# A gated recurrence on one core: h @ wh as sums of three bf16 numbers, the x side as plain products

## The chip, the core and the metric

The kernel runs on one core of one Trainium2 chip. The metric is the device time of one launch in microseconds (us); three runs of the kernel before gave a median of 1659.17 us (1657.54 to 1660.16).

## The reference

A recurrence over T = 512 steps for a batch of 8 with 512 inputs and 512 state units; all is float32.

```python
def step(h, x_t):
    fused = jax.nn.sigmoid(jnp.concatenate([x_t, h], axis=-1) @ w_W + w_b)
    hidden_state, output_state = jnp.split(fused, 2, axis=-1)
    memory_state = x_t @ wx_W + wx_b + hidden_state * (h @ wh_W + wh_b)
    h_new = output_state * h + (1.0 - output_state) * jnp.tanh(memory_state)
    return (h_new, h_new)
out = x + scan(step, cond_1024, x)
```

Below, r is the first gate (hidden_state), z the second (output_state). Each step needs four products with 512 x 512 matrices of the new state or input: h with the gates' two blocks, h with wh, x with the same three. Only the products with x can be made ahead of time.

## The kernel before, in words

**Layout.** State and inputs lie transposed, units on the 128 partitions, in four blocks k = 0 to 3 of 128 units; the contraction runs over k. Half A of the state is k = 0, 1, half B is k = 2, 3. Outputs are cut into four strips j of 32 PSUM partitions: a product (`mm`, L193) takes 32 columns of state as its stationary operand (8 of them hold the step's batch, the other 24 are zero, one group of 8 rows for each of four steps s) and streams the weights, so that four products, one for each strip j, stand side by side in the array. Four steps make a group g, with one set of PSUM banks for each of two groups in turn.

**A step on TensorE** (L372 to L384). `ORDER` (L27) names the groups of four products: A (192 columns: wh for half A, z and r for half A), B (128: r and wh of half B), C (64: z of half B), each for k = 0 to 3, in the order A0 B0 A1 A2 A3 B1 B2 B3 C0 C1 C2 C3. Then one slot of the x side's products for a later group (`take`, L384). The banks have been filled with the x side's sums by ScalarE copies (`spread`, L254), and the products add to them.

**The x side** (`products`, L293). For each pair of groups the 2 x 2 blocks of x and weights are combined as in a fast matrix product with seven products instead of eight: weight sums `tw` (`weight_sum`, L271, made once), x sums `sx` on POOL (`x_sum`, L282), and additions and copies on VectorE and ScalarE that put the parts together (L493 to L547), over eight steps in a hand-written order.

**A step on the other engines** (L458 to L483), for half A, then half B. VectorE transposes the gate's and wh's columns from PSUM to SBUF in 32 x 32 blocks (`turn_r`, `turn_h`, `turn_z`), ScalarE takes the sigmoids, and a scan on VectorE (`memory`, L447) multiplies and adds over two slots for each unit: r times (h @ wh), plus x's part. ScalarE's Tanh follows, and a second scan (`update`, L453) over three slots (h; n - h; times 1 - z plus h) gives the new state. `memory` and `update` are made for each block of 128 units, so twice in each half. All engines work in order. Two small memsets (`idle`, L432, L556) fill places of VectorE. ScalarE copies the state once more into the first slot (L483). POOL adds x to the state for the output (`add`, L557), SP loads x and stores the output in chunks of 16 steps (`load_x`, L106; `store`, L565), the last chunk in two parts.

The names and lines that the prediction uses: `mm` L194 (all matmuls), scans L390, sigmoid and Tanh L224, transposes L406 and L422, output additions on POOL L558, the x side's VectorE additions L495, L528, L534.

Of the kernel before, what the change touches and what calls it, by code (L numbers as in the profile page):

```python
# [16 lines left out]
B = 8  # L17
HU = 64

DVE_FILL = 23
IDLE = 3
LAST = 4
SYNC = mybir.DependencyInfo(mybir.DependencyClass.Sync, mybir.DependencyReason.DATA)

ORDER = "A0 B0 A1 A2 A3 B1 B2 B3 C0 C1 C2 C3"  # L27

FIRST = "A0 x A1 x A2 x A3 B0 B1 B2 B3 C0 C1 C2 C3"

BANKS = {"A": 192, "B": 128, "C": 64}

HALF = 192

WIDE = 384

SUMS = ((2,), (2,), (2, 1), (2, 1), (1,), (1, 3), (3,), (3, 3))

Q01, Q23 = slice(0, 64), slice(64, 128)

COLS = slice(64, 448)

XP = {"A": slice(0, 192), "X": slice(192, 320), "C": slice(320, 384), "B": slice(384, 512)}
# [3 lines left out]
def tile_cond_rnn_residual(  # L47
# [7 lines left out]
    wb3_d: bass.AP,  # L55
# [4 lines left out]

# [13 lines left out]

# [56 lines left out]

    wa = const.tile([P, NQ, NQ, 192], F32, name="wa")
    for k in range(NQ):
        nc.sync.dma_start(out=wa[:, k], in_=wa_d[k])
    wb = const.tile([P, NQ, NQ, 192], F32, name="wb")
    nc.sync.dma_start(out=wb[:, :3], in_=wb_d)
    nc.sync.dma_start(out=wb[:, 3], in_=wb3_d)

    def wh(bank, k, j):
        return wa[:, k, j] if bank == "A" else wb[:, k, j, {"C": slice(0, 64), "B": slice(64, 192)}[bank]]  # L140
# [3 lines left out]
    def pair(n, name, rows, slots):  # L144

        return const.tile([P, 2, rows, slots], F32, name=name).rearrange("p c n s -> p n c s")

    NH = 2 * GS  # L150
    hT = [[pair(n, f"hT{n}{i}", 32, 3) for i in range(NH)] for n in "AB"]

    md0 = [[pair(n, f"md0{n}{i}", 32, 2) for i in range(2)] for n in "AB"]
    md1 = [[pair(n, f"md1{n}{i}", 32, 2) for i in range(2)] for n in "AB"]
    hd0 = [[pair(n, f"hd0{n}{i}", B, 3) for i in range(2)] for n in "AB"]
# [11 lines left out]
    for n, t_ in enumerate(hd0[0] + hd0[1] + md0[0] + md0[1] + hT[0] + hT[1]):  # L167
        (nc.vector if n < DVE_FILL else nc.gpsimd).memset(t_, 0.0)
    for t_ in hd0[0] + hd0[1]:
        nc.gpsimd.memset(t_[:, :, :, 1], -1.0)  # L170
    idle = const.tile([P, IDLE], F32, name="idle")

    tw = [const.tile([P, 2, 2, WIDE], F32, name=f"tw{n}") for n in range(4)]
    sx = [[const.tile([P, 2, GS * B], F32, name=f"sx{n}{q}") for q in range(2)] for n in range(4)]
    step_bias = const.tile([P, HALF], F32, name="stepbias")
    xs = [const.tile([P, 512], F32, name=f"xs{n}") for n in range(2)]
    u2 = const.tile([P, WIDE], F32, name="u2")
    u3 = const.tile([P, WIDE], F32, name="u3")
    both = const.tile([P, WIDE], F32, name="both")

    def state(hf, i, slot=2):

        s = i % GS
        return hT[hf][i % NH][:, B * s : B * s + B, :, slot]

    ctx.enter_context(tc.manual_schedule())
    banks = [
        {n: psum.tile([P, w], F32, name=f"{n}{q}") for n, w in BANKS.items()}
        for q in range(2)
    ]  # L190
    xps = [psum.tile([P, 512], F32, name=f"xp{q}") for q in range(2)]

    def mm(out_, lhsT, rhs, start=False):  # L193
        nc.tensor.matmul(  # L194
            out_, lhsT, rhs, start=start, stop=False, skip_group_check=True
        )


    for t_ in list(banks[0].values()) + list(banks[1].values()):
# [10 lines left out]
    for t_ in xs:  # L210
        for c_ in (slice(0, 64), slice(448, 512)):
            nc.gpsimd.tensor_copy(t_[:, c_], bias[:, c_])
    for hf in range(2):
        for slot in (0, 2):
            nc.vector.tensor_copy(
                state(hf, 0, slot), hin[:, 2 * hf : 2 * hf + 2].rearrange("p c b -> p b c")
            )


# [9 lines left out]

    def seed(g):  # L230

        nc.scalar.copy(xps[g % 2][:, COLS], bias[:, COLS])

    def prefill(g):

        c, t0 = divmod(g * GS, TC)
        for k in range(NQ):
            for j in range(NQ):
                mm(
                    xps[g % 2][32 * j : 32 * j + 32, 64:448],  # L240
                    x_of(c, k, t0, GS),
                    wx[:, k, j, :],
                )
            yield

    def prefill_two():
        yield from prefill(2)
        yield from prefill(3)

    def source(g):  # L250

        return xs[g % 2] if g else xps[0]

    def spread(g, names):  # L254

        for n in names:
            nc.scalar.copy(banks[g % 2][n], source(g)[:, XP[n]])

    def turn_x(g, e):

        c0 = XP["X"].start + 32 * e
        nc.vector.transpose(md1[e // 2][g % 2][:, :, e % 2, 1], source(g)[:, c0 : c0 + 32])

    def wx_of(kh, nh):
        return wx[:, 2 * kh : 2 * kh + 2, 2 * nh : 2 * nh + 2]

    def x_half(o, n, kh):

        return x_of(o // 2, slice(2 * kh, 2 * kh + 2), 8 * (o % 2) + GS * n, GS)

    def weight_sum(n, k=slice(0, 2), j=slice(0, 2)):  # L271

        a, b = [
            (wx_of(0, 1), wx_of(0, 0)),
            (wx_of(1, 1), tw[0]),
            (wx_of(1, 1), wx_of(0, 1)),
            (wx_of(1, 0), tw[1]),
        ][n]
        at = (slice(0, P), k, j)
        nc.vector.tensor_tensor(tw[n][at], a[at], b[at], ALU.subtract)  # L280

    def x_sum(o, n):  # L282

        t_ = [q[o % 2] for q in sx]
        a, b, op = [
            (x_half(o, 1, 0), x_half(o, 1, 1), ALU.add),
            (t_[0], x_half(o, 0, 0), ALU.subtract),
            (x_half(o, 0, 0), x_half(o, 1, 0), ALU.subtract),
            (x_half(o, 0, 1), t_[1], ALU.subtract),
        ][n]  # L290
        nc.gpsimd.tensor_tensor(t_[n], a, b, op)

    def products(o):  # L293

        t_ = [q[o % 2] for q in sx]
        p1 = (0, x_half(o, 0, 0), wx_of(0, 0))
        p2 = (0, x_half(o, 0, 1), wx_of(1, 0))
        p3 = (0, t_[3], wx_of(1, 1))
        p4 = (1, x_half(o, 1, 1), tw[3])
        p6 = (0, t_[1], tw[1])  # L300
        p7 = (1, t_[2], tw[2])

        def pair(left, right, k, c0=0, c1=WIDE):
            for j in range(NQ):
                bank, lhs, rhs = left if j < 2 else right
                mm(
                    xps[bank][32 * j : 32 * j + 32, COLS.start + c0 : COLS.start + c1],
                    lhs[:, k],
                    rhs[:, k, j % 2, c0:c1],
                    start=right is p7 and k == 0 and j >= 2,  # L310
                )

        def shared(k):
            for j in range(NQ):
                c0 = HALF * (1 - j // 2)
                mm(
                    xps[j // 2][32 * j : 32 * j + 32, COLS.start : COLS.start + HALF],
                    t_[0][:, k],
                    tw[0][:, k, j % 2, c0 : c0 + HALF],
                )  # L320

        pair(p1, p7, 0)
        yield
        pair(p1, p7, 1)
        yield
        pair(p2, p6, 0)
        yield
        pair(p2, p6, 1)
        yield
        pair(p4, p3, 0, 0, 288)  # L330
        yield
        pair(p4, p3, 0, 288)
        shared(0)
        yield
        shared(1)
        pair(p4, p3, 1, 0, 96)
        yield
        pair(p4, p3, 1, 96)
        yield
# [7 lines left out]
    def x_side():  # L347
        for o in range(2, NG // 2):
            yield from products(o)

    seed(1)
    take(prefill(0))
    warm()
    later = x_side()
    first = {1: prefill(1), 2: prefill_two()}
    weight_sum(0)
    spread(0, "BCA")
    for e in range(NQ):
        turn_x(0, e)

    pool_done = {}
    summed = []
    for i in range(T):
# [5 lines left out]
        if t == 0:  # L369
            ot = out_p.tile([P, TC, NQ, B], F32, tag="ot", name=f"ot_{c}")  # L370

# [285 lines left out]
```

## Time and profile before

| | |
|---|---|
| runs, median of 3 | 1659.17 us |
| span of the profiled execution | 1659.2 us |
| that execution's first to last steady VectorE transpose of half A (510 steps) | 22.59 to 1654.18 us |
| DMA over the span | 31.16 MB, mean 19 GB/s |
| instruction fetch, largest queue | 424 packets, 6.95 MB |

The span runs from the first to the last instruction of one execution, and the durations used below are of that execution. PE is TensorE's matmuls and PEld its weight loads, which overlap them; DVE is VectorE, ACT is ScalarE, POOL is GpSimd, SP is SyncE, which issues most DMAs. A timeline row gives the start, the time from there to the group's end, the engine, the line, the operation, out<-in, sizes (partitions x elements, type), the count, and in brackets the idle time before it with what ended it. A f32 product leaves two matmul rows and two weight loads in the trace. Rows of one tile are merged, so a row with x8 covers eight matmuls of one k.

### The profile page before, as it was taken

To read this page: it belongs to the slowest core of one execution; us is meant where nothing else is said; L and a number is where in the kernel's file an instruction comes from. 1 tells how busy PE (TensorE), PEld (TensorE's weight loads), DVE (VectorE), ACT (ScalarE), POOL (GpSimd) and SP (SyncE) were. 2 spreads that over 40 slices of the span, in tenths; PEclk is the share of its full clock that TensorE was granted. 3 is DMA by queue.
4 is the path that set the end of the run, shared out by engine and by line. 5 is a ranking of instruction groups with operands and counts; after the bars stand their busy time and mean duration, and the time that the engine had idled before them with its cause. 6 is when DMAs were issued, how large, how long until landed. Compare 5 with 4: busy or idle time off the path is not lost.

```text
span 1659.2 us, 126037 instructions
## 1 busy us (share of the span) xinstructions
PE 1647.1 (99%) x54254; PEld 1484.3 (89%) x54254; DVE 1298.5 (78%) x9702; ACT 1106.9 (67%) x5884; POOL 325.6 (20%) x1284
## 2 busy tenths in 40 slices
PE   8999999999999999999999999999999999999998
PEld 5899999999999888899999999988899999999997
DVE  6877777777777777777777777777777777777776
ACT  4666666666666666666666666666666666666665
POOL 2221121211211212112112121121121211211211
PEclk9999999999999999999999999999999999999999
DMA  4000000000000000000000000000000000000000
GB/s 180 17 5 18 17 18 18 17 6 18 17 17 18 5 18 18 18 18 5 18 18 18 18 12 10 18 17 18 18 5 18 17 18 18 5 17 11 11 11 10
DMA packets 11512, 31.16 MB, mean 19 GB/s; under 512 B 1220, under 2 KB 1732, under 8 KB 10824
## 3 DMA queue, kind: packets, MB, share of 16 engines
q1 hardware_dynamic: 10800, 22.94, 4.0%
q8 instruction: 424, 6.95, 1.8%
q14 instruction: 136, 1.11, 0.2%
q10 hardware_dynamic: 152, 0.16, 0.0%
HBM read 14.70 MB, written 8.39 MB: 14 GB/s over the span
## 4 chain that ended last, share of the span: by engine, by line
PE 98%; DMA 1%; DVE 1%; issue 0%; ACT 0%; SPq 0%
PE A L194 40%; PE B L194 26%; PE xp L194 18%; PE C L194 13%; DMA wb<-in_wb_dram 1%; DMA wx<-in_wx_dram 0%; DVE tr L406 0%; DVE m L390 0%; DVE tz L406 0%; DVE hTA L390 0%; DVE md1A L422 0%; DVE md1B L422 0%; ACT hTB L224 0%; SPq L130 0%; DVE hTB L390 0%
## 5 line engine op out<-in xcount | busy, mean ns | idle before, releaser
L194 PE MATMUL A<-wa,hTA 128*32 128x192 f32 x8176 | 555.5, 327 | 2.7 <-DVE hTA L390 2.7
L194 PE MATMUL B<-wb,hTA 128*32 128x128 f32 x8192 | 453.0, 273 | 0.9 <-DMA wb<-in_wb_dram 0.9
L194 PE MATMUL A<-wa,hTB 128*32 128x192 f32 x8176 | 446.6, 326 | 0.0
L194 PEld LDWEIGHTS A<-wa,hTA 128*32 128x32 f32 x8176 | 290.7, 122 | 128.4 <-DVE hTA L390 107.1
L558 POOL TENSOR_TENSOR ot<-xin,hTB 128x16 f32<-128x16 f32 x503 | 125.6, 250 | 1292.4 <-DVE hTB L390 1281.8
L194 PEld LDWEIGHTS B<-wb,hTA 128*32 128x32 f32 x8192 | 346.8, 122 | 10.8 <-DMA wb<-in_wb_dram 1.3
L194 PE MATMUL B<-wb,hTB 128*32 128x128 f32 x8192 | 338.6, 273 | 0.1
L194 PEld LDWEIGHTS A<-wa,hTB 128*32 128x32 f32 x8176 | 324.3, 122 | 15.5 <-DVE hTB L390 0.3
L224 ACT ACTIVATE md0A<-tr 128x16 f32<-128x16 f32 x512 | 112.3, 219 | 314.4 <-DVE tr L406 314.4
L406 DVE STREAM_TRANSPOSE tr<-A 128x64 f32<-128x64 f32 x511 | 127.7, 250 | 214.3 <-PE A L194 199.3
L194 PE MATMUL xp<-tw,sx 128*32 128x384 f32 x1984 | 274.2, 406 | 0.3 <-issue 0.3
L194 PEld LDWEIGHTS B<-wb,hTB 128*32 128x32 f32 x8192 | 261.1, 122 | 0.4 <-DMA wb<-in_wb_dram 0.4
L390 DVE TENSOR_TENSOR_SCAN hTB<-hd0B,hTB 128x24 f32<-128x24 f32 x1024 | 157.8, 195 | 100.5 <-ACT hTB L224 100.5
L194 PE MATMUL C<-wb,hTB 128*32 128x64 f32 x8192 | 230.0, 219 | 0.1
L194 PE MATMUL C<-wb,hTA 128*32 128x64 f32 x8192 | 229.1, 219 | 0.0
L194 PE MATMUL xp<-wx,xin 128*32 128x384 f32 x1056 | 210.1, 486 | 0.0
L194 PEld LDWEIGHTS C<-wb,hTA 128*32 128x32 f32 x8192 | 206.6, 122 | 0.0
L390 DVE TENSOR_TENSOR_SCAN hTA<-hd0A,hTA 128x24 f32<-128x24 f32 x1024 | 190.9, 186 | 0.0
L194 PEld LDWEIGHTS C<-wb,hTB 128*32 128x32 f32 x8192 | 179.5, 122 | 0.6 <-issue 0.4
L224 ACT ACTIVATE hd0B<-tz 128x16 f32<-128x16 f32 x512 | 115.7, 226 | 94.8 <-DVE tz L406 94.8
L224 ACT ACTIVATE hTB<-hTB 128x16 f32<-128x16 f32 x512 | 120.1, 235 | 79.2 <-DVE hTB L390 70.3
L224 ACT ACTIVATE hTA<-m 128x8 f32<-128x8 f32 x1024 | 160.8, 206 | 2.5
(98 smaller groups left out, 2710.0 us busy)
## 6 DMA issues: line engine op xcount, KB each, us to landing
xin<-in_x_dram SPq DMA_DIRECT2D x31, 256.0 KB, 3.3
out_dram<-ot SPq DMA_DIRECT2D x31, 256.0 KB, 2.1
wx<-in_wx_dram SPq DMA_DIRECT2D x4, 768.0 KB, 7.1
wa<-in_wa_dram SPq DMA_DIRECT2D x4, 384.0 KB, 9.1
wb<-in_wb_dram SPq DMA_DIRECT2D x1, 1152.0 KB
wb<-in_wb_dram SPq DMA_DIRECT2D x1, 384.0 KB, 11.2
out_dram<-ot SPq DMA_DIRECT2D x1, 192.0 KB, 2.1
head<-in_xh_dram ACTq DMA_DIRECT2D x1, 144.0 KB, 5.0
```

Of the source, the lines that this page charges most:

```text
L194: nc.tensor.matmul(out_, lhsT, rhs, start=start, stop=False, skip_group_check=True)
L224: inst = nc.scalar.activation(out_, in_, func, **kw).ins
L390: return nc.vector.tensor_tensor_scan(*[t_[:, :, c_].rearrange("p n c s -> p (n c s)") for t_ in (out_, d0, d1)], 0.0, ALU.mult, ALU.add,).ins
L406: inst = nc.vector.transpose(t_.rearrange("p c n -> p (c n)"), raw[n][hf]).ins
L558: return engine.tensor_tensor(ot[:, t, 2 * hf : 2 * hf + 2, :].rearrange("p c n -> p n c"), x_of(c, slice(2 * hf, 2 * hf + 2), t, 1).rearr ...
```

## The change

- The gates' products with h stay f32, but in two banks of 128 columns (A: z and r of half A; B: z and r of half B).
- The product with wh is made in bf16. Each weight is written as a sum of three bf16 numbers (`split`, once, before step 0). The state too: its upper 16 bits, the upper 16 bits of the rest, and those of what then remains. The three parts of the 8 batch rows lie beside each other as 24 columns of one stationary tile (`pieces`), so one product with a weight part gives three groups of 8 rows in PSUM; with three weight parts there are three products for each k and strip, 64 columns wide, for each half (G is wh of half A, H of half B). The three row groups are summed in the `memory` scan, which now has five slots for each unit: three parts, the bias, and x's part, which is added after the multiplication with r.
- ScalarE copies the state into the first row group; POOL makes the two subtractions and the copy of the state into slot 0.
- The x side has no combined blocks: `prefill` makes one k of the plain product, 384 columns wide, in each step, for the group after the next. The combining additions and copies, weight sums, x sums and idle memsets go.
- One transpose (`turn_gates`) takes z and r of a half together, and one (`turn_x`) x's part of a whole group.
- The last chunk is stored in one part.

The diff, cut to its core:

```diff
-ORDER = "A0 B0 A1 A2 A3 B1 B2 B3 C0 C1 C2 C3"
+NP = 3
+SL = 5
+ROWS = NP * B
+ORDER = "A0 A1 B0 B1 A2 A3 G0 G1 G2 G3 B2 B3 H0 H1 H2 H3"
...
+    banks = [{n: psum.tile([P, 128], F32, name=f"{n}{q}") for n in "AB"} for q in range(2)]
+    hbanks = {n: psum.tile([P, HU], F32, name=f"H{n}") for n in "AB"}
...
+    def first_piece(hf, i):
+        act(("p", hf, i % 2), pieces[hf][i % 2][:, :, :B], state(hf, i), AF.Copy)
+
+    def other_pieces(hf, i):
+        t_ = pieces[hf][i % 2]
+        hi = t_.bitcast(BF16)[:, :, 1::2]
+        nc.gpsimd.tensor_tensor(t_[:, :, B : 2 * B], state(hf, i), high(hf, i), ALU.subtract)
+        nc.gpsimd.tensor_tensor(
+            t_[:, :, 2 * B : 3 * B], t_[:, :, B : 2 * B], hi[:, :, B : 2 * B], ALU.subtract
+        )
+
+    def again(hf, i):
+        nc.gpsimd.tensor_copy(state(hf, i, 0), state(hf, i))
...
     def prefill(g):
         c, t0 = divmod(g * GS, TC)
         for k in range(NQ):
             for j in range(NQ):
+                mm(xps[g % 2][32 * j : 32 * j + 32, :384], x_of(c, k, t0, GS), wx[:, k, j, :])
             yield
+    def spread(g, n):
+        nc.scalar.copy(banks[g % 2][n], xps[g % 2][:, {"A": XA, "B": XB}[n]])
+    def turn_x(g):
+        nc.vector.transpose(md1[g % 2][:, :, :, SL - 1], xps[g % 2][:, XX])
...
+    def split(k):
+        w = whf[:, k].rearrange("p j (h n) -> p j h n", h=2)
+        t_ = work.tile([P, NQ, 2, HU], F32, tag="split", name=f"split{k}")
+        nc.scalar.copy(whp[:, k, :, :, 0], w)
+        nc.vector.tensor_tensor(t_, w, whp[:, k, :, :, 0], ALU.subtract)
+        nc.scalar.copy(whp[:, k, :, :, 1], t_)
+        nc.vector.tensor_tensor(whp[:, k, :, :, 2], t_, whp[:, k, :, :, 1], ALU.subtract)
...
+        if s == 0 and g + 2 < NG:
+            later[g] = prefill(g + 2)
+            seed(g + 2)
+        for n in ORDER.split():
             bank, k = n[0], int(n[1])
+            if bank in "AB":
+                w = (wa if bank == "A" else wb)[:, k]
+                hs = cells(k // 2, i)[:, k % 2, :, 2]
+                for j in range(NQ):
+                    mm(ps[bank][32 * j : 32 * j + 32, :], hs, w[:, j])
+            else:
+                hf = "GH".index(bank)
+                to = hbanks["AB"[hf]]
+                hs = pieces[k // 2][i % 2].bitcast(BF16)[:, k % 2, 1 : 2 * ROWS : 2]
+                for p in range(NP):
+                    for j in range(NQ):
+                        mm(to[32 * j : 32 * j + ROWS, :], hs, whp[:, k, j, hf, p], start=k == p == 0)
+        if g in later:
+            take(later[g], 1)
...
+        def turn_gates(hf):
+            t_ = work.tile([P, 4, 32], F32, tag=f"t{hf}", name=f"t{hf}_{i}")
+            nc.vector.transpose(t_.rearrange("p c n -> p (c n)"), ps["AB"[hf]])
+            tz[hf] = t_
+            act(("r", hf, g % 2, s), md0[g % 2][:, 2 * hf : 2 * hf + 2, rows, SL - 1], t_[:, 2:, rows], AF.Sigmoid)
+            act(("zc", hf, i % 2), hd0[hf][i % 2][:, :, :, 2], t_[:, :2, rows], AF.Sigmoid, scale=-1.0)
+
+        def turn_h(hf):
+            nc.vector.transpose(
+                md1[g % 2][:, 2 * hf : 2 * hf + 2, rows, : SL - 1].rearrange("p c n s -> p c s n"),
+                hbanks["AB"[hf]],
+            )
...
+        turn_gates(0)
+        turn_h(0)
+        memory(0, 0)
+        memory(0, 1)
+        turn_gates(1)
+        update(0, 0)
+        update(0, 1)
+        turn_h(1)
+        grown(0)
+        memory(1, 0)
+        memory(1, 1)
+        update(1, 0)
+        update(1, 1)
+        grown(1)
...
+        if s == 0 and g + 1 < NG:
+            turn_x(g + 1)
+        if s in (1, 2) and g + 1 < NG:
+            spread(g + 1, "AB"[s - 1])
+        for hf in range(2):
+            add(hf, t, 1, nc.gpsimd if i < T - 1 else nc.vector)
```

`grown(hf)` calls `first_piece`, `other_pieces` and `again` for the next step's state. On VectorE the first `memory` scan behind each `turn_h` waits for that transpose's own result, and on POOL the second subtraction waits for the first.

More of the change, by code (lines that the diff above doesn't have):

```diff
@@ L54, in tile_cond_rnn_residual @@
     wb_d: bass.AP,
-    wb3_d: bass.AP,
+    wh_d: bass.AP,
     bias_d: bass.AP,
@@ L142, in tile_cond_rnn_residual @@
-    load_x(0, 1)
[L144 to L155, printed above, removed]
+        nc.sync.dma_start(out=whf[:, k], in_=wh_d[k])
@@ L156, in tile_cond_rnn_residual @@
+    md0 = [const.tile([P, NQ, 32, SL], F32, name=f"md0{q}") for q in range(2)]
+    md1 = [const.tile([P, NQ, 32, SL], F32, name=f"md1{q}") for q in range(2)]
+    hd0 = [[const.tile([P, 2, B, 3], F32, name=f"hd0{n}{i}") for i in range(2)] for n in "AB"]
+    pieces = [[const.tile([P, 2, 32], F32, name=f"pc{n}{i}") for i in range(2)] for n in "AB"]
     zeros = const.tile([P, 512], F32, name="zeros")
@@ L209, in tile_cond_rnn_residual @@
     nc.vector.tensor_copy(bias, xps[0])
[L210 to L217, printed above, removed]
+    for hf, n in enumerate("AB"):
+        nc.vector.tensor_copy(hbanks[n], bias[:, 384 + HU * hf : 384 + HU * hf + HU])
     written = {}
@@ L228, in act @@
         return inst
+    def first_piece(hf, i):
[10 more added lines that the diff above has]
+    for hf in range(2):
+        nc.vector.tensor_copy(state(hf, 0), hin[:, 2 * hf : 2 * hf + 2])
+        first_piece(hf, 0)
+        other_pieces(hf, 0)
+        again(hf, 0)
     def seed(g):
-        nc.scalar.copy(xps[g % 2][:, COLS], bias[:, COLS])
+        nc.scalar.copy(xps[g % 2][:, :384], bias[:, :384])
     def prefill(g):
@@ L259, in turn_x @@
[L259 to L339, printed above, removed]
@@ L345, in take @@
             n = None if n is None else n - 1
-    def x_side():
-        for o in range(2, NG // 2):
-            yield from products(o)
-    seed(1)
[L352 to L362, printed above, removed]
+    def split(k):
[5 more added lines that the diff above has]
+        nc.vector.tensor_tensor(whp[:, k, :, :, 2], t_, whp[:, k, :, :, 1], ALU.subtract)
+    seed(0)
+    take(prefill(0))
+    seed(1)
+    take(prefill(1))
+    spread(0, "A")
+    spread(0, "B")
+    turn_x(0)
+    for k in range(NQ):
+        split(k)
+    later = {}
     for i in range(T):
@@ L381, in tile_cond_rnn_residual @@
-        if 1 <= i < 4:
-            take(first[2], 2 if i == 3 else 3)
-        else:
-            take(later if i else first[1], 1)
+            if bank in "AB":
[10 more added lines that the diff above has]
+                        mm(to[32 * j : 32 * j + ROWS, :], hs, whp[:, k, j, hf, p], start=k == p == 0)
@@ L442, in tile_cond_rnn_residual @@
-        ms = [
-            work.tile([P, 2, B, 2], F32, tag=f"m{hf}", name=f"m{hf}_{i}").rearrange("p c n s -> p n c s")
-            for hf in range(2)
-        ]
+        tz = {}
+        def turn_gates(hf):
[4 more added lines that the diff above has]
+            act(("zc", hf, i % 2), hd0[hf][i % 2][:, :, :, 2], t_[:, :2, rows], AF.Sigmoid, scale=-1.0)
@@ L447, in memory @@
+        def turn_h(hf):
+            nc.vector.transpose(
+                md1[g % 2][:, 2 * hf : 2 * hf + 2, rows, : SL - 1].rearrange("p c n s -> p c s n"),
+                hbanks["AB"[hf]],
+            )
+        ms = [work.tile([P, 2, B, SL], F32, tag=f"m{hf}", name=f"m{hf}_{i}") for hf in range(2)]
         def memory(hf, q):
-            c_ = slice(q, q + 1)
-            scan(c_, ms[hf], md0[hf][g % 2][:, rows], md1[hf][g % 2][:, rows])
-            act(("n", hf, q, i % NH), state(hf, i, 1)[:, :, c_], ms[hf][:, :, c_, 1], AF.Tanh)
+            scan(ms[hf][:, q], md0[g % 2][:, 2 * hf + q, rows], md1[g % 2][:, 2 * hf + q, rows])
+            act(("n", hf, q, i % 8), state(hf, i, 1)[:, q], ms[hf][:, q, :, SL - 1], AF.Tanh)
@@ L453, in update, with grown @@
         def update(hf, q):
             s1 = (i + 1) % GS
-            new = hT[hf][(i + 1) % NH][:, B * s1 : B * s1 + B]
-            return scan(slice(q, q + 1), new, hd0[hf][i % 2], hT[hf][i % NH][:, rows])
-        turn_r(0)
+            new = cells(hf, i + 1)[:, q, B * s1 : B * s1 + B]
+            scan(new, hd0[hf][i % 2][:, q], cells(hf, i)[:, q, rows])
+        def grown(hf):
+            if i < T - 1:
+                first_piece(hf, i + 1)
+                other_pieces(hf, i + 1)
+                again(hf, i + 1)
@@ L481, in tile_cond_rnn_residual @@
         update(1, 1)
-        for hf in range(2):
-            act(("h", hf, (i + 1) % NH), state(hf, i + 1, 0), state(hf, i + 1), AF.Copy)
+        grown(1)
         if i < 3:
             load_x(i + 1)
-        o, u = divmod(i, 2 * GS)
-        nxt, two = o + 1 < NG // 2, o + 2 < NG // 2
-        if i == 0:
-            nc.scalar.copy(xs[1][:, COLS], xps[1][:, COLS])
-            spread(1, "B")
-            turn_x(1, 0)
-        add_ = nc.vector.tensor_tensor
-        if u == 3 and o and nxt:
-            add_(xs[0][Q23, COLS], xps[0][Q23, COLS], both[Q23], ALU.add)
-        elif u == 7 and two:
-            nc.vector.tensor_copy(xs[0][Q01, COLS], xps[0][Q01, COLS])
-        elif u == 0 and o and nxt:
-            add_(u3[Q23], xps[1][Q23, COLS], u2[Q23], ALU.add)
```

254 lines of the change are left out of this document (50 added, 204 removed).

## The prediction

> **What bounds the kernel now.** First the page's engine shares, the granted clock and the shares of the chain that ended last.
>
> ```profile
> span 1659.2 us, 126037 instructions
> PE 1647.1 (99%) x54254; PEld 1484.3 (89%) x54254; DVE 1298.5 (78%) x9702; ACT 1106.9 (67%) x5884; POOL 325.6 (20%) x1284
> PEclk9999999999999999999999999999999999999999
> PE 98%; DMA 1%; DVE 1%; issue 0%; ACT 0%; SPq 0%
> PE A L194 40%; PE B L194 26%; PE xp L194 18%; PE C L194 13%; DMA wb<-in_wb_dram 1%; DMA wx<-in_wx_dram 0%; DVE tr L406 0%; DVE m L390 0%; DVE tz L406 0%; DVE hTA L390 0%; DVE md1A L422 0%; DVE md1B L422 0%; ACT hTB L224 0%; SPq L130 0%; DVE hTB L390 0%
> ```
>
> TensorE works 99% of the span at full clock, and the chain is matmuls alone: every other engine is hidden behind the four kinds of products. So I need two things: what TensorE's own work per step becomes, and whether the others still fit behind it. The timeline of one step in the middle gives the first: the distance between the starts of successive groups.
>
> ```profile
> 800.44 0.54 PE L194 MATMUL A<-wa,hTA 128*32 128x192 f32 x8
> 800.77 0.43 PE L194 MATMUL B<-wb,hTA 128*32 128x128 f32 x8
> 800.98 0.54 PE L194 MATMUL A<-wa,hTA 128*32 128x192 f32 x8
> 801.31 0.86 PE L194 MATMUL A<-wa,hTB 128*32 128x192 f32 x16
> 801.96 0.43 PE L194 MATMUL B<-wb,hTA 128*32 128x128 f32 x8
> 802.18 0.65 PE L194 MATMUL B<-wb,hTB 128*32 128x128 f32 x16
> 802.61 0.43 PE L194 MATMUL C<-wb,hTA 128*32 128x64 f32 x16
> 802.84 0.43 PE L194 MATMUL C<-wb,hTB 128*32 128x64 f32 x16
> 803.06 0.49 PE L194 MATMUL xp<-wx,xin 128*32 128x384 f32 x2
> 803.71 0.54 PE L194 MATMUL A<-wa,hTA 128*32 128x192 f32 x8
> ```
>
> Eight rows are one k: four column strips side by side, two passes each. Width 192 takes 0.33 us (800.44 to 800.77), 128 takes 0.22 (801.96 to 802.18), 64 takes 0.11 (802.61 to 802.84 holds two k), the x part of this step 0.65 (803.06 to 803.71). A strip's pass therefore costs 0.83 ns a column and about 2.5 ns besides. Four k are 4 x (0.325 + 0.218 + 0.112) = 2.62 us. The x part is 0.65 in this step; its eight slots hold 7/8 of the plain product, so 0.57 on the mean: 3.19 us a step.
>
> **The change, on TensorE.** Gates: eight groups of width 128, 8 x 0.218 = 1.74 us. The x side, plain again: one k of width 384, 0.65. The product with wh leaves f32: 24 bursts of four bf16 products, 64 columns wide. No steady row is bf16; the first rows of the span are, at another pace:
>
> ```profile
> 2.20 0.31 PE L194 MATMUL B<-none 128*128 128x128 bf16 x1
> 2.31 0.26 PE L194 MATMUL C<-none 128*128 128x64 bf16 x1
> 2.38 0.35 PE L194 MATMUL A<-none 128*128 128x192 bf16 x1
> 2.70 3.60 PE L194 MATMUL xp<-zeros 128*128 128x512 f32 x4
> ```
>
> Width 128 in bf16 takes 0.11 us there (2.20 to 2.31), 0.83 ns a column; the f32 rows of 512 take some 0.85 each, 1.66 a column. A bf16 column costs half an f32 one, so at the steady pace 64 columns take 27 + 2.5 = 29 ns. Bounds: the bf16 row of 64 takes 0.07 (2.31 to 2.38), 35 ns at the steady pace; the f32 pass of the same width takes 56, and no row shows that a weight load hides behind less. I take 29, since f32 passes of all widths are set by their columns alone. 24 x 0.029 = 0.70. TensorE's sum: 1.74 + 0.65 + 0.70 = **3.09 us**, 0.10 less than before; at 35 ns 3.23, at 56 ns 3.73.
>
> The Trainium skill, "TensorE: Matmul & The Clock Gate", section "Wait — 56ns, not 53.3ns?", says that start-to-start of matmuls never falls below some 25 ns however narrow they are. Held for all four strips together, 96 products would cost 2.4 us in place of 0.70. The C rows speak against that: 16 in 0.23 us are 14 ns each.
>
> **The change, on the other engines.** Removed: the x side's combining additions and copies on VectorE, ScalarE and POOL. They are hidden now, so their going gains nothing. Moved: A0 A1 B0 B1 need half A's state alone, A2 half B's, G0 half A's pieces, G2 half B's pieces. Added, per half: two POOL subtractions and a POOL copy, and a scan over 40 elements instead of 16. The steady step's rows give the delays:
>
> ```profile
> 800.13 0.20 DVE L390 TENSOR_TENSOR_SCAN hTA<-hd0A,hTA 128x24 f32<-128x24 f32 x1
> 800.38 0.23 PEld L194 LDWEIGHTS A<-wa,hTA 128*32 128x32 f32 x8 [0.27 <-DVE hTA L390]
> 800.68 0.31 ACT L224 ACTIVATE hTB<-m 128x8 f32<-128x8 f32 x2
> 800.93 0.31 DVE L390 TENSOR_TENSOR_SCAN hTB<-hd0B,hTB 128x24 f32<-128x24 f32 x2 [0.20 <-ACT hTB L224]
> 801.32 0.25 POOL L558 TENSOR_TENSOR ot<-xin,hTB 128x16 f32<-128x16 f32 x1 [2.39 <-DVE hTB L390]
> 801.52 0.25 POOL L558 TENSOR_TENSOR ot<-xin,hTA 128x16 f32<-128x16 f32 x1
> 802.22 0.25 DVE L406 STREAM_TRANSPOSE tr<-A 128x64 f32<-128x64 f32 x1
> 802.39 0.21 DVE L422 STREAM_TRANSPOSE md1A<-A 128x64 f32<-128x64 f32 x1
> 802.50 0.22 ACT L224 ACTIVATE md0A<-tr 128x16 f32<-128x16 f32 x1 [1.00 <-DVE tr L406]
> 802.75 0.28 DVE L390 TENSOR_TENSOR_SCAN m<-md0A,md1A 128x16 f32<-128x16 f32 x2
> 802.95 0.23 DVE L406 STREAM_TRANSPOSE tr<-B 128x64 f32<-128x64 f32 x1
> 803.10 0.21 DVE L422 STREAM_TRANSPOSE md1B<-B 128x64 f32<-128x64 f32 x1
> 803.50 0.17 DVE L390 TENSOR_TENSOR_SCAN hTA<-hd0A,hTA 128x24 f32<-128x24 f32 x1
> 803.59 0.25 DVE L390 TENSOR_TENSOR_SCAN m<-md0B,md1B 128x16 f32<-128x16 f32 x2
> ```
>
> Hand-overs: VectorE to TensorE 0.05 (scan ends 800.33, loads 800.38); VectorE to ScalarE 0.03 (802.47, 802.50); ScalarE to VectorE as little; VectorE to POOL 0.08 (scans end 801.24, POOL 801.32); TensorE to VectorE 0.26 after the next group's start (B starts 801.96, tr 802.22). Spacing on VectorE: a 64-wide transpose 0.15 (802.95 to 803.10), so one of 128 about 0.22; a scan of 16 0.08 (the pair at 803.59 ends after 0.25, one lasting 0.17), of 24 0.09 (803.50 to 803.59). A scan of 40 isn't in the trace: between nothing and 2 ns per added element, 0.08 to 0.14 in spacing and 0.17 to 0.22 in length. I take the upper ends, from the 16-to-24 step at its largest. A POOL operation on 16 elements takes 0.25. A wait of an engine for its own semaphore isn't shown either: I take the hand-over into that engine, 0.03 on VectorE, 0.08 on POOL; nothing at the least, about 0.1 at the most.
>
> Now a new loop closes through POOL: half B's pieces release G2, G3 releases VectorE, and VectorE works strictly in order. From G2:
> - G2, G3: 6 bursts 0.175; to turn_h(0) 0.26; its transpose and the wait for its own result 0.25: 0.685
> - memory(0,0), (0,1): 2 x 0.14: 0.965
> - turn_gates(1), 128 wide, B3 long done: 0.22: 1.185
> - update(0,0) 0.12 (the Tanh spacing), update(0,1) 0.11: 1.415
> - turn_h(1) 0.25, memory(1,0) 0.14, memory(1,1) 0.22 + 0.03: 2.055
> - Tanh 0.20 + 0.03, update(1,1) 0.19 + 0.08 to POOL: 2.555
> - two subtractions 0.25 + 0.08, 0.25 + 0.05 to TensorE: 3.185
> - the weight load before G2's first product, 0.03: **3.21 us**
>
> ScalarE's first piece lies beside the subtractions, which read the state itself. So the loop is 0.12 longer than TensorE's 3.09: the cover is gone, TensorE waits ahead of G2, and behind that wait stand G3, B2, B3, H and the x products. The other waits fit: B3 ends 0.61 after G2, and H and x put A0 at 1.61; update(0,1), 0.18 long, has handed over by 1.185 + 0.12 + 0.18 + 0.05 = 1.535. A2 at 2.48 waits some 0.05 for update(1,1), which G2's wait takes in. ScalarE's seeds and spreads fall into its idle time between half B's first piece and the next gates. SP keeps a load and a store for each chunk; only the last store grows, from 4 steps to 16, inside the 5 us at the end below.
>
> One more price is the port that POOL shares with VectorE's scans:
>
> ```profile
> 804.47 0.55 DVE L528 TENSOR_TENSOR xs<-xp,u 64x384 f32<-64x384 f32 x1
> 804.62 0.25 POOL L558 TENSOR_TENSOR ot<-xin,hTA 128x16 f32<-128x16 f32 x1
> 807.75 0.62 DVE L534 TENSOR_TENSOR xs<-u,both 64x384 f32<-64x384 f32 x1
> 807.91 0.56 POOL L558 TENSOR_TENSOR ot<-xin,hTA 128x16 f32<-128x16 f32 x1
> ```
>
> Beside an addition with both inputs in SBUF (L534) POOL needs 0.56 instead of 0.25, and VectorE 0.62 against 0.55. Half A's subtractions now lie beside scans of half B, with two such inputs. On VectorE nothing to 0.07 a step; I take 0.04: **3.25 us a step**.
>
> **Start and end.** The rows of the first and last steady transposes:
>
> ```profile
> 22.59 0.25 DVE L406 STREAM_TRANSPOSE tr<-A 128x64 f32<-128x64 f32 x1
> 1654.18 0.25 DVE L406 STREAM_TRANSPOSE tr<-A 128x64 f32<-128x64 f32 x1 [0.95 <-PE A L194]
> ```
>
> Step 1 begins to turn at 22.6, 510 steps lie between (3.20 each), and 5 us follow the last step's turn. Now wh's split into three pieces stands before step 0: four rounds of copy, subtraction, copy, subtraction. Nothing to 6 us; I take 2. So 24.5 + 510 x 3.25 + 5 = **1687 us**, against this execution's 1659.2; the median of the runs is 1659.17, the same. The break-even step is (1659.2 - 29.5) / 510 = 3.195.
>
> **Rivals.**
> - *The loop stays hidden* (faster). The scans cost hardly more than those of 16: four places on the loop, up to 0.05 each, take it to 3.01, under TensorE's 3.09. Decides if the loop is 0.12 shorter than my sum. For it: a scan of 24 is spaced like one of 16. Against: the pairs at 802.75 and 800.93 are looser. 29.5 + 510 x 3.09 = 1605, up to 1650 with a loop in between.
> - *POOL's queue.* Half A's two subtractions and copy stand ahead of half B's. By the sums above they end 0.86 after update(0,1), and half B's turn comes at 1.07: 0.21 of slack. With each held by a scan for up to 0.15, they overrun it by 0.1 to 0.24: 3.31 to 3.45 a step, 1718 to 1789. The skill says the same of the port ("Advanced Engine Details and Errata", section "GPSIMD Details": POOL shares an interface with VectorE and conflicts with instructions of two SBUF inputs); the row at 807.91 agrees, with 0.56 for 0.25.
> - *Narrow products don't reach 29 ns*, because the load of 24 columns doesn't hide. TensorE decides from 34 ns on; at 40 ns 3.35 us a step, 1738; at 56 ns 3.73, 1932.
> - *The floor of 25 ns over all strips*: 4.79 us a step, 2472. Hardly, by the C rows.
>
> **How the numbers follow.** My forecast, the loop with steps of 3.2 to 3.31 us (1661 to 1718), has 0.45. The hidden loop has 0.25, POOL's queue 0.15, slow narrow products 0.10, the floor 0.01, a tie by chance 0.04. About 0.2% is what a measurement of this kernel can tell from no change. Faster is the hidden loop, 0.25; within 0.2%, 0.04; slower the rest, 0.71. The range runs from the hidden loop's 1605 to 1830, which takes in POOL's queue and narrow products up to about 45 ns.
>
> **What would show it.** Right: TensorE's share falls to about 95%, with some 0.16 us a step idle ahead of the loads from half B's pieces, released by POOL; six bursts of H in 0.175 us; on VectorE the first scan after turn_h starts 0.25 behind it. The hidden loop: no wait ahead of G2, TensorE at 99%. POOL's queue: POOL operations of half A longer than 0.25, and half B's first subtraction starting later than 0.08 after update(1,1). Slow products: bursts spaced over 34 ns with no wait. Wrong in any case: a wait ahead of A0, or of G0.

## The result, and the profile after

The changed kernel takes **2519.68 us** (median of 4 runs, 2517.62 to 2528.74), the kernel before 1659.66 (4 runs, 1657.54 to 1661.81). The ratio is 1.519, with a 95% interval of 1.516 to 1.522. The prediction was 1687 us with a range from 1605 to 1830: the sign was right, and the size was far outside the range. The profiled execution has a span of 2526.9 us; less the 29.5 us of start and end that the prediction took, that is 4.90 us a step in place of 3.20.

First the page of the changed kernel: the engines' shares, the granted clock, the packets of the instruction queue, and the chain that ended last.

```profile
span 2526.9 us, 193353 instructions
PE 1905.2 (75%) x86028; PEld 1524.1 (60%) x86028; DVE 1303.3 (52%) x6305; ACT 1016.4 (40%) x5514; POOL 793.7 (31%) x4110
...
PEclk9999999999999999999999999999999999999999
...
q8 instruction: 676, 11.08, 1.8%
...
PE 64%; issue 25%; DVE 7%; POOL 3%; DMA 1%; ACT 0%; DVEq 0%; POOLq 0%; SPq 0%; ACTq 0%
```

No engine is full any more: TensorE, at 99% before, is down to 75%, and VectorE, ScalarE and POOL are lower still. The clock is as before. The chain gives 25% of the span to "issue", time in which an engine waited for nothing that the profile shows; before it was 0%. So for a quarter of the span neither columns nor a semaphore holds the kernel, and the q8 row has grown from the 424 packets in the table of before to 676.

The timeline of TensorE shows where the idle time lies. The last number before the bracket is the count of matmul rows; a float32 product leaves two of them, a bf16 product one, and each comes with a weight load.

```profile
1200.97 0.27 PE L148 MATMUL B<-wb,hTB 128*32 128x128 f32 x1 [0.44 <-issue]
1200.97 0.35 PE L148 MATMUL HB<-whp,pcA 128*24 128x64 bf16 x21
1201.15 0.20 PE L148 MATMUL HB<-whp,pcB 128*24 128x64 bf16 x3
1201.16 0.19 PE L148 MATMUL HB<-whp,pcA 128*24 128x64 bf16 x1
1201.18 0.20 PE L148 MATMUL HB<-whp,pcB 128*24 128x64 bf16 x2
1201.19 0.19 PE L148 MATMUL HB<-whp,pcA 128*24 128x64 bf16 x1
1201.19 0.19 PE L148 MATMUL HB<-whp,pcB 128*24 128x64 bf16 x1
1201.22 0.19 PE L148 MATMUL HB<-whp,pcA 128*24 128x64 bf16 x1
1201.25 0.37 PE L148 MATMUL HB<-whp,pcB 128*24 128x64 bf16 x18
1201.43 0.88 PE L148 MATMUL xp<-wx,xin 128*32 128x384 f32 x8
1202.10 0.65 PE L148 MATMUL A<-wa,hTA 128*32 128x128 f32 x16
1202.54 0.65 PE L148 MATMUL B<-wb,hTA 128*32 128x128 f32 x16
1203.01 0.66 PE L148 MATMUL A<-wa,hTB 128*32 128x128 f32 x16
1203.48 0.35 PE L148 MATMUL HA<-whp,pcA 128*24 128x64 bf16 x23
1204.59 0.20 PE L148 MATMUL HA<-whp,pcA 128*24 128x64 bf16 x1 [0.76 <-issue]
1204.71 0.36 PE L148 MATMUL HA<-whp,pcB 128*24 128x64 bf16 x24
```

Add the counts from the first stall (1200.97) to the row before the second (1204.59): 1 + 21 + 3 + 1 + 2 + 1 + 1 + 1 + 18 + 8 + 16 + 16 + 16 + 23 = 128 matmuls, with 128 weight loads: **256 instructions**. The second stall falls in the middle of a burst, between two products of the same bank with the same stationary tile, so it has nothing to do with what the product reads. Where TensorE does run, it runs as the prediction priced it: the 24 products from 1204.71 to 1204.89 take 0.18 us, 0.030 for a burst of four.

The view of the DMA traffic of the 10 us from 1200 on, in which TensorE's rows stall at 1200.97, 1204.59 and 1208.43:

```profile
DMA packets 3, 0.05 MB, mean 5 GB/s; under 512 B 0, under 2 KB 0, under 8 KB 0
...
q8 instruction: 3, 0.05, 1.9%
```

Three packets, three stalls. The row's 1.9% of 16 engines' 10 us is 3.0 us for three packets, so the transfer of one takes about 1.0 us of the 3.6 to 3.8 from stall to stall (worked out from this row); the rest passes outside it. Over the whole span 11.08 MB in 676 packets are 16.4 KB a packet, and the program counts agree: 86,028 matmuls and as many loads are 172,056 instructions, 672 times 256. So q8 is the queue that brings TensorE its instructions.

Two rows of the changed kernel's waits (us in total, times, longest) answer signs that the prediction named:

```profile
PEld A L148 <- DVE hTA L266: 120.8, 313, 0.9
PEld L148 <- POOL pcB L180: 1.3, 5, 0.4
```

The wait for half B's pieces, which the prediction put at 0.16 us in every step, is hardly there: 1.3 us in the whole run. The wait ahead of A0, named as proof against the prediction, is there in 313 of the 512 steps; with 120.8 us it is small beside the 25% of "issue", some 630 us.

**Theory F**: TensorE's instructions arrive 256 at a time, one such packet can't be had more often than about every 3.6 to 3.7 us, and the changed kernel asks for 336 instructions a step (36 float32 products of four, 96 bf16 products of two) where the one before asked for some 212. Rivals: **L**, the dependency loop of the prediction was mis-sized and sets 4.9 us; **N**, the prediction's own rival with a floor of 25 ns for each narrow product, 2472 us, which came within 2% of the result; and a price for switching between float32 and bf16.

### The profile page after: what moved, and what is told of

Read it like the earlier page. It is cut to its first block, busy times and chain, and to the rows that moved or that the text cites. A ratio compares the mean times of both kernels' runs of the same rounds, so it can differ in the third digit from the quotient of the medians.

```text
span 2526.9 us, 193353 instructions
## 1 busy us (share of the span) xinstructions
PE 1905.2 (75%) x86028; PEld 1524.1 (60%) x86028; DVE 1303.3 (52%) x6305; ACT 1016.4 (40%) x5514; POOL 793.7 (31%) x4110
## 3 DMA queue, kind: packets, MB, share of 16 engines
q8 instruction: 676, 11.08, 1.8%
## 4 chain that ended last, share of the span: by engine, by line
PE 64%; issue 25%; DVE 7%; POOL 3%; DMA 1%; ACT 0%; DVEq 0%; POOLq 0%; SPq 0%; ACTq 0%
PE A L148 18%; PE B L148 16%; PE xp L148 11%; PE HA L148 11%; PE HB L148 8%; DVE m L266 2%; DVE md L280 2%; DVE hTA L266 1%; DVE hTB L266 1%; POOL pcA L180 1%; POOL pcA L179 1%; DVE t L274 1%; POOL hTA L185 1%; DMA whf<-in_wh_dram 0%; DMA xin<-in_x_dram 0%
## 5 line engine op out<-in xcount | busy, mean ns | idle before, releaser
L148 PE MATMUL xp<-wx,xin 128*32 128x384 f32 x4032 | 459.5, 496 | 45.5 <-issue 45.5
L148 PEld LDWEIGHTS <-pcA 128*24 128x24 bf16 x24576 | 401.4, 93 | 145.6 <-issue 140.3
L148 PEld LDWEIGHTS <-pcB 128*24 128x24 bf16 x24576 | 333.0, 91 | 256.0 <-issue 241.5
L167 ACT ACTIVATE md<-t 128x16 f32<-128x16 f32 x1024 | 237.8, 232 | 566.6 <-DVE t L274 566.0
L266 DVE TENSOR_TENSOR_SCAN m<-md,md 128x40 f32<-128x40 f32 x2048 | 386.2, 230 | 109.6 <-DVE md L280 2.7
L148 PE MATMUL A<-wa,hTA 128*32 128x128 f32 x8192 | 368.7, 276 | 87.3 <-issue 75.8
L148 PE MATMUL A<-wa,hTB 128*32 128x128 f32 x8192 | 382.1, 280 | 31.3 <-issue 17.0
L148 PE MATMUL HB<-whp,pcB 128*24 128x64 bf16 x12288 | 229.7, 196 | 153.6 <-issue 153.6
L148 PE MATMUL HA<-whp,pcB 128*24 128x64 bf16 x12288 | 225.7, 195 | 74.2 <-issue 64.2
L148 PE MATMUL HA<-whp,pcA 128*24 128x64 bf16 x12288 | 235.7, 194 | 47.3 <-issue 45.2
```

What stands on the lines that cost most here:

```text
L148: nc.tensor.matmul(out_, lhsT, rhs, start=start, stop=False, skip_group_check=True)
L167: inst = nc.scalar.activation(out_, in_, func, **kw).ins
L266: return nc.vector.tensor_tensor_scan(*[t_.rearrange("p n s -> p (n s)") for t_ in (out_, d0, d1)], 0.0, ALU.mult, ALU.add).ins
```

## The experiments

The kernel before, run again on the chips of these experiments, took between 1659.3 and 1663.8 us. A time below is of one run unless a number of runs stands with it. "A step" is the profiled span less 29.5 us, over 510.

### Instructions added to the kernel before

```diff
-                mm(to[32 * j : 32 * j + 32, :], hs, wh(bank, k, j))
+                if bank == "A":
+                    for c0 in (0, 96):
+                        mm(to[32 * j : 32 * j + 32, c0 : c0 + 96], hs, wh(bank, k, j)[:, c0 : c0 + 96])
+                else:
+                    mm(to[32 * j : 32 * j + 32, :], hs, wh(bank, k, j))
```

> The kernel before, with each of the 16 products of bank A, 192 columns wide, issued as two of 96 columns: the same columns are streamed, no bf16 product and no POOL piece is there, but 64 TensorE instructions a step are added: 276 instead of 212. F: 276/256 x 3.56 to 3.74 = 3.84 to 4.03 us a step, 24.5 + 510 x that + 5 = 1988 to 2085 us. Against F (N, L, or a cost of switching between float32 and bf16): nothing of theirs is in this kernel, so 1660 to 1700 us.

Measured: 2074.97 us. The kernel before, with the same columns and none of the change in it, is 25% slower for 64 more instructions a step: 4.01 us a step, as F had it. The second dose splits bank B too:

> The kernel before with the products of bank A (192 columns) and of bank B (128) each issued as two halves: the same columns, 340 TensorE instructions a step, four more than the changed kernel has. F: 340/256 x 3.71 to 3.80 = 4.93 to 5.05 us a step, 2542 to 2604 us, as slow as the changed kernel without any part of the change. A price for a product or a switch of type instead: bank A's split alone cost 0.81 us a step for 16 more products, and a price for narrow products would fall more on B's halves of 64 columns than on A's of 96; by a plain price per product 4.81 us, 2483 us.

Measured: 2549.25 us, in F's interval and 66 us above a plain price per product; it is as slow as the changed kernel, 1.2% above it. The page of that kernel:

```profile
span 2547.5 us, 191573 instructions
PE 1905.4 (75%) x87022; PEld 1679.0 (66%) x87022; DVE 1340.4 (53%) x9702; ACT 1120.7 (44%) x5884; POOL 324.9 (13%) x1284
...
q8 instruction: 680, 11.14, 1.9%
...
PE 73%; issue 25%; DVE 1%; DMA 1%; ACT 0%; POOL 0%; SPq 0%
```

It looks like the page of the changed kernel: TensorE 75%, issue 25%, 680 packets. A price of narrow bf16 products (N), of a switch of type, or of POOL's loop (L) can't be in it. How fast TensorE got through its instructions is best read from the busy time and counts of a stretch from 600 to 1000 us; each row gives the stretch and its length, then busy time and count (x...) of TensorE's matmuls, of its weight loads, of VectorE, ScalarE and POOL. The kernel before, the changed one, and the ones with bank A and with A and B split:

```profile
600.00:1000.00 400.00, 400.00 (x13296) 361.16 (x13290) 316.06 (x2365) 271.46 (x1443) 78.78 (x314) 1.00 0.05 15
```

```profile
600.00:1000.00 400.00, 302.47 (x13721) 243.12 (x13713) 204.83 (x994) 160.61 (x873) 125.20 (x648) 1.00 0.04 11
```

```profile
600.00:1000.00 400.00, 359.50 (x13836) 316.88 (x13830) 257.41 (x1891) 218.13 (x1155) 62.57 (x250) 1.00 0.05 13
```

```profile
600.00:1000.00 400.00, 298.53 (x13672) 264.13 (x13668) 209.23 (x1518) 176.16 (x926) 50.41 (x202) 1.00 0.04 11
```

Three kernels with steps of 4.90, 4.01 and 4.94 us pass 13,672 to 13,836 matmuls, and as many loads, in the same 400 us: 3.70 to 3.75 us for 256 instructions. The kernel before passed 13,296, which is 3.85 us: it stood 3 to 4% below this limit while its TensorE showed 99%.

### The loop through POOL taken away

```diff
                 first_piece(hf, i + 1)
-                other_pieces(hf, i + 1)
                 again(hf, i + 1)
```

> The changed kernel without the two subtractions on POOL of each half (the second and third row group keep what the first step left there, so the output isn't the reference's): the products and their number are unchanged, but the bursts no longer wait for POOL's pieces. F: the instruction count is unchanged at 336 a step, 4.67 to 4.91 us, so 2420 to 2530 us, within 2% of the changed kernel. L: two subtractions of 0.22 us with a gap of 0.08 leave the loop, so at least 0.5 us a step of 4.88 goes: 2260 us or less. N: unchanged, as F.

Measured: 2510.20 us, 0.4% less. The two subtractions on POOL of each half, and with them the wait ahead of G2, can go and the time moves by 0.4%. L falls: a loop through POOL does not set the 4.9 us.

### Fewer products in the changed kernel

```diff
-                for p in range(NP):
+                for p in range(2):
```

> The changed kernel with two of the three weight parts in the products of G and H (the third part is left out of the sum, so the output is less exact): 64 bf16 products a step instead of 96, 272 TensorE instructions a step instead of 336 (a float32 product counts as four, a bf16 one as two). Theory F, TensorE's instructions arrive in packets of 256 and one packet takes 3.56 to 3.74 us all told (the spacing of the packets in the changed kernel): 272/256 x 3.56 to 3.74 = 3.78 to 3.97 us a step, 24.5 + 510 x that + 5 = 1958 to 2057 us. Rival N, each narrow product takes 25 ns by itself and the strips don't overlap: 2.39 + 64 x 0.025 = 3.99, 2064 us; this run alone doesn't tell it from F. Rival L, the dependency loop through POOL was mis-sized and sets 4.88 us a step: the loop holds six bursts before turn_h, which lose 0.06 us, so 4.82 us, 2490 us.

Measured: 2096.08 us, 39 above F's interval: 548 packets in a span of 2094.3 us are 3.82 us each, near the 3.70 to 3.75 of the kernels above but over it. Instructions are no longer all that holds this kernel, as a row of its waits shows:

```profile
PEld A L148 <- DVE hTA L266: 207.3, 428, 1.2
```

In 428 of the 512 steps A0 waits for the state of half A, 207.3 us in all, where it was 313 and 120.8 in the changed kernel. The next kernel, with `range(1)` in place of `range(2)`, shows where that wait comes from.

> The changed kernel with one of the three weight parts (the other two are left out of the sum): 32 bf16 products and 208 TensorE instructions a step, about as many as the kernel before (212). F: the packets allow 208/256 x 3.56 to 3.74 = 2.89 to 3.04 us, so the loop of the prediction comes to light: 3.25 less 0.12 us for the four bursts that it loses = 3.13 us, 1626 us; 1600 to 1680. N: 2.39 + 32 x 0.025 = 3.19, 1656, not to be told from F here. L: 4.88 - 0.12 = 4.76 us, 2457 us.

Measured: 1841.87 us, 3.55 a step. F's part holds: the stalls all but go, and the page has only 420 packets in 1840.1 us, 4.38 us each. But the loop that comes to light is 0.4 us longer than I had expected. Its timeline, with the waits of the step in brackets:

```profile
1200.73 0.40 PEld L148 LDWEIGHTS A<-wa,hTA 128*32 128x32 f32 x16 [0.82 <-DVE hTA L266]
...
1201.93 0.40 PEld L148 LDWEIGHTS A<-wa,hTB 128*32 128x32 f32 x16 [0.36 <-DVE hTB L266]
...
1202.12 0.22 POOL L179 TENSOR_TENSOR pcB<-hTB 128x16 f32<-128x16 f32 x1 [0.48 <-DVE hTB L266]
...
1202.42 0.21 POOL L180 TENSOR_TENSOR pcB<-pcB 128x16 f32<-128x16 f32 x1
...
1202.66 0.32 DVE L274 STREAM_TRANSPOSE t<-A 128x128 f32<-128x128 f32 x1 [0.36 <-PE A L148]
1202.68 0.12 PEld L148 LDWEIGHTS <-pcB 128*24 128x24 bf16 x8 [0.16 <-POOL pcB L180]
...
1202.98 0.31 DVE L280 STREAM_TRANSPOSE md<-HA 128x64 f32<-128x64 f32 x1
...
1203.39 0.37 DVE L266 TENSOR_TENSOR_SCAN m<-md,md 128x40 f32<-128x40 f32 x2
...
1203.69 0.29 DVE L274 STREAM_TRANSPOSE t<-B 128x128 f32<-128x128 f32 x1
...
1203.99 0.31 DVE L266 TENSOR_TENSOR_SCAN hTA<-hd0A,hTA 128x24 f32<-128x24 f32 x2
```

Half B's state lets A2 start (1201.93); A3's end lets turn_gates(0) start (1202.66); turn_h(0), the scans, turn_gates(1) and the updates follow it on VectorE one behind the other. TensorE stands 0.82 us ahead of A0 and 0.36 ahead of A2. The wait that the prediction put into the loop, ahead of G2, is there, released by POOL, but it is 0.16 us and turn_gates(0) has started by then. How much of it is POOL's is told by the same kernel without the subtractions:

> The changed kernel with one weight part and without the two POOL subtractions (two parts and two row groups are left out of the sum): 208 instructions a step, 2.62 us of columns. F: the loop is out of the way, and the packets are the floor: 2.89 to 3.04 us, 1503 to 1580 us, with waits for instructions every 256 of them. If no floor of instructions existed, TensorE's columns would: 2.62 us, 1366 us, or a loop through VectorE and ScalarE somewhere between.

Measured: 1780.37 us, 3.43 a step, 0.12 less. Neither packets (416 in 1778.6 us, 4.28 each) nor columns (2.62 a step) set it, against my expectation. Its waits show a loop through TensorE and VectorE, closed in every step:

```profile
PEld A L148 <- DVE hTA L266: 466.4, 515, 1.6
DVE t L274 <- PE A L148: 307.6, 510, 1.3
```

POOL adds only 0.12 us to it, and these rows, to be held against 1202.66 to 1203.39 above, show where:

```profile
1200.86 0.32 DVE L274 STREAM_TRANSPOSE t<-A 128x128 f32<-128x128 f32 x1 [0.68 <-PE A L148]
...
1201.10 0.27 DVE L280 STREAM_TRANSPOSE md<-HA 128x64 f32<-128x64 f32 x1
...
1201.47 0.38 DVE L266 TENSOR_TENSOR_SCAN m<-md,md 128x40 f32<-128x40 f32 x2
```

turn_h(0) starts 0.24 us behind turn_gates(0) in place of 0.32, and the scan 0.37 behind turn_h(0) in place of 0.41.

### Fewer instructions for the same sum

Three kernels keep all columns and the whole sum and merge products, so that fewer instructions are issued; the cuts show their main lines. In the first G and H are merged, in one bank:

```diff
-ORDER = "A0 A1 B0 B1 A2 A3 G0 G1 G2 G3 B2 B3 H0 H1 H2 H3"
+ORDER = "A0 A1 B0 B1 A2 A3 G0 G1 B2 B3 G2 G3"
...
-                        mm(to[32 * j : 32 * j + ROWS, :], hs, whp[:, k, j, hf, p], start=k == p == 0)
+                        mm(hb[32 * j : 32 * j + ROWS, :], hs, whp[:, k, j, p], start=k == p == 0)
```

> The changed kernel with the products of G and H merged: one bf16 product of 128 columns for each k, part and strip, into one bank, instead of two of 64. The same columns are streamed and the whole sum is computed; 48 bf16 products and 240 TensorE instructions a step instead of 336. F: 240/256 x 3.56 to 3.74 = 3.34 to 3.51 us a step, 1732 to 1818 us, unless the loop, which now holds bursts twice as wide (six of 0.058 instead of 0.029: + 0.17 us on 3.25 = 3.42), comes out above it. N: 48 products of at least 53 ns (128 columns at full clock, from 0.218 us for a burst of 128 float32 columns in four passes) with no overlap of strips: 2.39 + 2.56 = 4.95, 2550 us. L: a loop of 4.88 us gets 0.17 longer: 2600 us.

Measured: 2225.97 us. In the second, A and B share a bank, and their products for k = 0 and 1 are merged as well (shown against the first):

```diff
-ORDER = "A0 A1 B0 B1 A2 A3 G0 G1 B2 B3 G2 G3"
+ORDER = "AB0 AB1 A2 A3 G0 G1 G2 G3 B2 B3"
...
+    abs_ = [psum.tile([P, 256], F32, name=f"AB{q}") for q in range(2)]
+    banks = [{"A": t_[:, :128], "B": t_[:, 128:], "AB": t_} for t_ in abs_]
```

> As the merged kernel, and the products of gate banks A and B for k = 0 and 1 merged as well, 256 columns wide into one bank (order AB0 AB1 A2 A3 G0 to G3 B2 B3): 24 float32 and 48 bf16 products a step and 4 of the x side, 208 TensorE instructions, fewer than the 212 of the kernel before. The whole sum is computed and the same columns are streamed. F: the packets allow 2.89 to 3.04 us; then TensorE's columns (3.09) or the loop (3.25 + 0.17 for wider bursts = 3.42) set the step: 1700 to 1800 us, 1774 if the loop is as sized. If the loop of the prediction is shorter than sized, down to 1606. L or N: above 2400 us.

Measured: 2345.38 us (4 runs), a ratio to before of 1.412 (1.410 to 1.415). Without the POOL subtractions:

> The kernel of 208 instructions (merged products of G and H, gates merged for k = 0 and 1) without the two subtractions on POOL of each half (row groups two and three keep their first values; the output isn't the reference's). This one sizes the loop: if the loop through POOL sets the step there, the step gets shorter by 0.3 to 0.6 us until TensorE's columns (3.09 us, 1605 us) or the packets (2.89 to 3.04 us) stop it. If packets or columns set the step already, the time stays within 1%.

Measured: 2341.97 us, within 1%. My expectation read that as packets or columns setting the step, and this is not so: 416 packets in 2340.2 us are 5.6 us each, and TensorE is busy for 77%. In the third the order of the change is kept, with merging for k = 0 and 1 alone (shown against the change):

```diff
-ORDER = "A0 A1 B0 B1 A2 A3 G0 G1 G2 G3 B2 B3 H0 H1 H2 H3"
+ORDER = "AB0 AB1 A2 A3 GH0 GH1 G2 G3 B2 B3 H2 H3"
```

> The changed kernel's own sum and order with fewer instructions where that leaves the loop nearly as it is: gates of A and B merged for k = 0 and 1 (AB0 AB1, 256 columns wide), products of G and H merged for k = 0 and 1 (128 wide), the rest as in the change (A2 A3, G2 G3, B2 B3, H2 H3). The whole sum is computed with the same columns; 256 TensorE instructions a step instead of 336. F: the runs that instructions held (the changed kernel, one part left out, bank A split) took 3.71 to 3.80 us for 256 of them, so 3.71 to 3.80 us a step; the loop that came to light with one part, 3.52 us, gets four bursts (0.12) and 0.06 longer: 3.70. Both end near 3.7 to 3.85 us: 1916 to 1995 us. If only the loop counted, 1890 to 1920. N, 25 ns for each narrow product: 2.39 + 72 x 0.025 = 4.19 us, 2166 us. L: unchanged near 2500 us.

Measured: 2282.83 us (4 runs), a ratio of 1.374 (1.371 to 1.376). All four are faster than the changed kernel, and packets hold none of them: the last has 516 in 2281.9 us, 4.42 us each, and its longest row of waits for instructions is

```profile
PEld xp L149 <- issue: 6.7, 17, 1.7
```

But the three with the whole sum are some 290 to 650 us slower than F and the loop made me expect. VectorE's timeline in the last of them:

```profile
1204.77 0.32 DVE L274 STREAM_TRANSPOSE t<-AB 128x128 f32<-128x128 f32 x1 [1.65 <-PE AB L149]
1205.01 0.29 DVE L280 STREAM_TRANSPOSE md<-H 128x64 f32<-128x64 f32 x1
1205.40 0.37 DVE L266 TENSOR_TENSOR_SCAN m<-md,md 128x40 f32<-128x40 f32 x2
```

And TensorE's of the same step:

```profile
1203.08 0.66 PE L149 MATMUL AB<-wab,hTB 128*32 128x128 f32 x16
...
1204.07 0.67 PE L149 MATMUL AB<-wab,hTB 128*32 128x128 f32 x16
```

The products of A2 and A3 begin at 1203.08, those of B2 and B3 at 1204.07 and end by 1204.74. turn_gates(0) needs A alone, but starts at 1204.77, when the last product into the shared bank has ended: the program orders the reads of a bank behind all products into it that stand ahead of them. In the kernel with one part, whose A and B lie in banks of their own, turn_gates(0) starts 0.73 us after A2 (1201.93 to 1202.66); here 1.69. Merging took the instructions away and put about a microsecond into the loop: the steps of the three are 4.30, 4.53 and 4.42 us, against 3.55 with one part. The Trainium skill, "PSUM — Partial Sum Buffer", section "PSUM bank collisions raise a hardware error", gives a reason for that order: two engines may not use one bank in the same partitions at the same time, not even in different columns. The wait here agrees with it; no run here shows what would happen without it. The second kernel pays it too; its group of these transposes has 874 us of idle time ahead of it, put down to products into the shared bank, and POOL's part of the loop no longer matters (0.15% without it). In the first kernel, where G2 and G3 stand behind B2 and B3, it is turn_h(0) that waits. The two group rows:

```profile
L273 DVE STREAM_TRANSPOSE t<-AB 128x128 f32<-128x128 f32 x1024 | 311.0, 304 | 874.7 <-PE AB L149 874.5
```

```profile
L279 DVE STREAM_TRANSPOSE md<-H 128x64 f32<-128x64 f32 x1024 | 298.3, 291 | 391.5 <-PE H L149 390.9
```

A merged bank without that wait was not tried, and neither was one load of a stationary tile for several products. None of these versions comes near the kernel before.

## Why the prediction was wrong, point by point

- **"TensorE's sum: 1.74 + 0.65 + 0.70 = 3.09 us, 0.10 less than before."** This is the step that failed. Where nothing stalls, each term came near what was taken (a burst 0.030 us for 0.029; from one group's start to the next, the 16 rows of A at 1202.10 take 0.44 for 0.44 and the x rows at 1201.43 0.67 for 0.65), but a sum of columns is not TensorE's time: I never counted the instructions. The change takes columns away and adds 124 instructions a step, and 336 of them at 3.70 to 3.75 us for 256 need 4.86 to 4.92 us; 4.90 was measured. The page of before held the count: 54,254 matmuls and as many loads, in the 424 packets of the table. It could not show that the rate was a limit, since columns hid it; but 672 packets at no better than the old 3.9 us are 2630 us, and that rival stood open beside the others.
- **Narrow products, and the floor of 25 ns.** The bursts refute both: 24 products in 0.18 us. The floor, held over all strips, gave 2472 us and came close by chance; the kernel with A and B split has no bf16 product in its loop and takes 2549.
- **"3.21 us", the loop, and 3.25 with the port.** It did not set the pace of the changed kernel, but it was too short: 3.55 us with one weight part, where these terms gave 3.13. The 128-wide transpose was taken at 0.22 and lasts 0.29 to 0.32; from turn_h(0) to the first scan I took 0.25 and the trace has 0.41, 0.31 of it the transpose into five slots. Only the POOL subtractions were cheaper than taken (0.22, and 0.08 for the wait of POOL for itself, as taken). And the loop closes through A2, A3 and turn_gates(0) more than through POOL and G2: 3.43 us are left without the POOL subtractions. The prediction named "a wait ahead of A0" as proof against it, and that wait is there: 0.82 us with one part, and in 313 steps of the changed kernel.
- **POOL's queue and the port.** No run showed them as the limit: without the subtractions the changed kernel takes 0.4% less.
- **The sign.** Slower had 0.71, for the loop's sake, and came true for another reason. If instructions had cost nothing, the loop of 3.55 us and four more bursts (0.12) would still have given about 29.5 + 510 x 3.67 = 1900 us; that is an estimate from the kernel with one part and was not measured.

## What to carry to other kernels

Count TensorE's instructions as well as its columns: in these kernels a float32 product was four and a bf16 product two, however narrow, and three unlike kernels that asked for more than 256 of them in 3.7 us got them no faster than that. A TensorE at 99% hides such a limit, so compare the packets of the instruction queue with the span before cutting wide products into narrow ones; and before merging them again, look which reads then wait for the whole bank.

## What the runs showed of the hardware that was not expected

- TensorE got 256 instructions per 3.70 to 3.75 us (13,672 to 13,836 matmuls with their loads in 400 us), whether they were float32 products of 64 to 384 columns or bf16 products of 64. The transfer of a packet is about 1.0 us of that in the 10 us shown; what the rest goes into is not settled here.
- The Trainium skill, "Runtime: NRT & Kernel Launch", section "Instruction fetch mechanics", says that instructions come in blocks of 16 KiB, 256 at a time, and that crossing a block is mostly hidden. The trace agrees on the block (128 matmuls and 128 loads from stall to stall, 16.4 KB a packet), and differs on the rest: 0.44 and 0.76 us of idle TensorE at two blocks in a row, a quarter of the span in all.
- The limit shows in a profile as "issue", with a bubble in the middle of a burst. In the kernel before, 3 to 4% short of it, the chain had 0% of that.
